# Two banded layers: the band in four 64x64 tiles with crossed channels, part of the inner norm on VectorE, and another order within a step

## The chip, the core and the metric

The kernel runs on one core of a Trainium2 chip. The metric is the device time of one execution in microseconds (us). It is given as the median of several runs of the same program. A profile is taken of one execution apart from these.

The core has five engines that run side by side, each with its own queue of instructions worked off in order: TensorE (PE in the profile; its weight loads are a row of their own, PEld), VectorE (DVE), ScalarE (ACT), GpSimd (POOL) and SyncE (SP), which here issues nearly all transfers. TensorE writes to PSUM, a memory of eight banks; a tile called "banks" takes two of them, a tile called "bank" takes one.

## The reference

The input is x of shape 1x512x512x64 in float32. Two identical layers with weights of their own act on it one after the other, each preceded by a group norm over pairs of channels. One layer, with WIN = 4, 64 channels in and 128 inside:

```
xn    = layernorm(x) * norm_scale + norm_bias
left  = (xn @ Wl + bl) * mask * sigmoid(xn @ Wlg + blg)
right = (xn @ Wr + br) * mask * sigmoid(xn @ Wrg + brg)
gate  = sigmoid(xn @ Wog + bog)
out[i, j, c] = sum over k = i-4 .. i+4 of  left[k, i, c] * right[k, j, c]
y     = (layernorm(out) * out_norm_scale + out_norm_bias) * gate @ Wo + bo
```

The sum over k is a banded matrix product for each of the 128 channels c: rows i of the result need rows i-4 to i+4 of `right`. The result of a layer is added to its input.

## The kernel before

**Rows and columns.** The 512 rows are cut into nine blocks of S = 64 rows that overlap by eight (`row_blocks`). A block's 512 columns come as two halves of 256, which stand on partitions 0 to 63 and 64 to 127 at the same time. A *chunk* is 128 columns of each half, so there are 18 chunks in a layer. A chunk is worked in 16 *units* of JU = 8 columns. The loop in `layer` (lines 765 to 847) makes one *step* t per unit. In one step, different units are in different stages.

**Stages.** A unit is loaded (`load`), gets the group norm (`affine`, two GpSimd operations over 128x512 elements), its statistics (`inner_stats`, VectorE) and the inner layer norm (`inner_norm`, lines 435 to 439, two GpSimd operations over 128x512). TensorE transposes it (`transposed`) and ScalarE copies the result from PSUM to the tile zT (`kept`, line 460), which is also stored to DRAM (`later`). `right` (line 487) projects a unit in two calls of four columns: TensorE, a sigmoid on ScalarE into `sg`, a product on VectorE into RO. `left` (line 497) does so for the nine diagonals that the band needs, once in each layer in its first steps, and writes them to DRAM (`left_of`).

**Band.** When a chunk's 16 units are in RO, `mix` (line 539) multiplies: one call takes HB = 8 channels, that is 16 calls in a chunk. A stationary operand is a 64x64 matrix of `left` for a channel, taken from a slab A of HA = 16 channels that `take_left` (line 527) has fetched; the moving operand is RO, 64 rows of 128 columns. Each call uses two 64x64 tiles of the array: rows 0 to 63 with output partitions 0 to 63, and rows 64 to 127 with output partitions 64 to 127. Half of a call's result goes back to RO by ScalarE, half by VectorE. The 16 calls fall on ten of a chunk's 16 steps: 2, 1, 2, 2, 1, 2, 1, 2, 2, 1 (line 729).

**Output.** Some 14 steps after a chunk is complete each unit goes out: `out_stats` (VectorE), `norm` (line 610, eight ScalarE operations), `gates` (line 622, TensorE and two sigmoids), `turned` (line 641: transposes, then the product with the gate on VectorE into ZH), `end` (line 673: output projection, VectorE's sum with the input XR, two stores). `biased` adds a constant to XR on GpSimd. In layer one `sums` collects channel sums on TensorE for the group norm of the next layer. `solve` (line 577), every fourth step, turns the variances of several units into reciprocal roots: a few small VectorE operations and some dozen small ones on GpSimd; `norm` and `inner_norm` of the next steps use its results (`nm`, `rs`).

**Order.** Everything issued through `en` keeps the order of the program text on its engine, so the lines of the loop are the queue order of each engine. Two tiles of two banks (`two_banks`) are shared, in turn, by the two calls of `right`, by `transposed` and by each `mix`; whoever takes one waits until the one before has been read out. Single banks (`one_bank`) go round among three in layer one and four in layer two. In the profile nearly every line of the loop is recorded as L373, the wrapper that keeps the order, so groups are told apart by their tiles.

Of the kernel before, what the change touches and what calls it, by code (L numbers as in the profile page):

```python
# [8 lines left out]
F32 = mybir.dt.float32  # L9
I32 = mybir.dt.int32  # L10
AF = mybir.ActivationFunctionType
# [5 lines left out]
P = 128  # L17
WIN = 4
# [7 lines left out]
HB = 8  # L26
HA = 16
# [52 lines left out]
def tile_two_banded_layers(  # L80
# [27 lines left out]

    slab = S * (S + 2 * WIN) * HA
    size = H // HA * slab  # L110
# [271 lines left out]
    class Unit:  # L382
# [4 lines left out]
        def __init__(self, at: int, blk: Block = None, j: int = 0, near: int = None):  # L387
            self.at, self.blk, self.j, self.near = at, blk, j, near

# [45 lines left out]
    def inner_norm(u: Unit):  # L435
        z = u.z.rearrange("p (k t) c -> p k t c", t=2)
        m = u.mean.unsqueeze(3).broadcast_to([P, JU // 2, 2, D])
        en.gpsimd.tensor_tensor(z, z, m, ALU.subtract)
        en.gpsimd.tensor_tensor(u.z, u.z, last(u.rs, D), ALU.mult)
# [20 lines left out]
    def kept(u: Unit):  # L460
        u.t = ztp.tile([P, JU // 2, P], F32, tag="zT", name="zT")
        to = u.t.rearrange("c k (n p) -> c n k p", n=2)
        for n, pt in enumerate(u.pt):
            en.scalar.activation(
                to[:, n : n + pt.shape[1]], pt.rearrange("c n (k p) -> c n k p", p=S),
                AF.Identity, bias=1.0,
            )
        if u.near is None:
            en.sync.dma_start(later[u.at], u.t)
# [5 lines left out]
    def projected(u: Unit, q: int, w: bass.AP):  # L475

        pr = two_banks().rearrange("p (e k h) -> p e k h", e=2, k=JQ // 2)
        for k in range(JQ // 2):
            for e in range(2):
                part = slice(e * D, (e + 1) * D)  # L480
                en.tensor.matmul(
                    pr[:, e, k, :], lhsT=u.t[part, q // 2 + k, :], rhs=w[part],
                    start=True, stop=True,
                )
        return pr

    def right(u: Unit, q: int, w: dict):
        pr = projected(u, q, w["right"]).rearrange("p e k h -> p (e k) h")
        sg = wk.tile([P, JQ, H], F32, tag="sg", name="sg", bufs=2)
        en.scalar.activation(sg, pr[:, :, H:], AF.Sigmoid)  # L490
        en.vector.tensor_tensor(
            RO[:, :, u.c + q : u.c + q + JQ, :],
            pr[:, :, :H].rearrange("p j (h t) -> p h j t", t=2),
            sg.rearrange("p j (h t) -> p h j t", t=2), ALU.mult,
        )

    def left(u: Unit, q: int, w: dict):

        n0 = u.near + q
        pr = projected(u, q, w["left"])  # L500
        sg = wk.tile([P, JQ, H], F32, tag="sg", name="sg", bufs=2)
        sl = sg.rearrange("p j h -> p (j h)").rearrange("p (s j x) -> p s j x", j=JQ, x=HA)
        sv = sl.rearrange("p s (k e) x -> p e k s x", e=2)
        for e in range(2):
            en.scalar.activation(
                sv[:, e], pr[:, e, :, H:].rearrange("p k (s x) -> p k s x", x=HA), AF.Sigmoid
            )
        near = w["near"][:, n0 : n0 + JQ].unsqueeze(1).unsqueeze(3)
        en.gpsimd.tensor_tensor(sl, sl, near.broadcast_to([P, H // HA, JQ, HA]), ALU.mult)
        for e in range(2):  # L510
            en.vector.tensor_tensor(
                sv[:, e], pr[:, e, :, :H].rearrange("p k (s x) -> p k s x", x=HA), sv[:, e],
                ALU.mult,
            )
        for o, r, k, m in runs(n0, n0 + JQ):
            for n, b in enumerate(blocks):
                q0 = b.s // JQ
                at = n * size + (r * (S + 2 * WIN + 1) + k) * HA
                en.sync.dma_start(
                    strided(  # L520
                        left_of, at, (JQ * (S + 2 * WIN + 1) * HA, S // JQ), (slab, H // HA),
                        (1, m * HA),
                    ),
                    sl[q0 : q0 + S // JQ, :, o : o + m, :].rearrange("q s j x -> q s (j x)"),
                )

    def take_left(n: int, h: int) -> bass.AP:


        A = lp.tile([P, S, HA], F32, tag="A", name="A")  # L530
        at = n * size + h * slab + WIN * HA
        for e in range(2):
            en.sync.dma_start(
                A[e * S : (e + 1) * S].rearrange("p i h -> p (i h)"),
                strided(left_of, at, ((S + 2 * WIN) * HA, S), (1, S * HA)),
            )
        return A

    def mix(c: int, A: bass.AP, h0: int):


        j0 = c % 2 * (JC - JW)
        R = RO[:, :, j0 : j0 + JC, :]
        pb = two_banks()
        ph = pb.rearrange("i (h j) -> i h j", j=JC)
        for turn in range(2):
            for h in range(HB // 2):
                for e in range(2):
                    part = slice(e * S, (e + 1) * S)
                    hh = (turn ^ e) * (HB // 2) + h  # L550
                    en.tensor.matmul(
                        ph[part, hh, :], lhsT=A[part, :, h0 % HA + hh],
                        rhs=R[part, (h0 + hh) // 2, :, hh % 2],
                        start=True, stop=True,
                    )
        q = HB // 4
        for n in range(2):
            o = R[:, h0 // 2 + n * q : h0 // 2 + (n + 1) * q]
            v = pb.rearrange("i (h t j) -> i h j t", t=2, j=JC)[:, n * q : (n + 1) * q]
            if n == 0:  # L560
                en.scalar.copy(o, v)
            else:
                en.vector.tensor_copy(o, v)
# [46 lines left out]
    def norm(o: Out):  # L610
        o.on = onp.tile([P, JU, H], F32, tag="on", name="on")
        for j in range(JU):
            en.scalar.activation(
                o.on[:, j, :].rearrange("p (h t) -> p h t", t=2), RO[:, :, o.c + j, :],
                AF.Identity, bias=o.nm[:, j : j + 1], scale=o.rs[:, j : j + 1],
            )
# [5 lines left out]
    def gates(o: Out, w: dict):  # L622
# [3 lines left out]
        for e, pg in enumerate(pgs):  # L626
            part = slice(e * D, (e + 1) * D)
            en.tensor.matmul(
                pg, lhsT=w["gate"][part],
                rhs=o.t[part].rearrange("c k (e p) -> c (k e) p", e=2)[:, :, b.lo : b.hi],  # L630
                start=True, stop=True,
            )
        g = gp.tile([H, 4 * JQ * (S - WIN)], F32, tag="gate", name="gate")
        for e, pg in enumerate(pgs):
# [6 lines left out]
    def turned(o: Out, w: dict):  # L641
# [10 lines left out]
        for n, pt in enumerate(pts):  # L652
# [20 lines left out]
    def end(dst: bass.AP, o: Out, w: dict):  # L673
        m = o.blk.m
        po = one_bank().rearrange("i (j c) -> i j c", c=D)
        for k in range(JQ):
            for e in range(2):
                for n in range(2):
# [5 lines left out]
                    )  # L684
        f = o.xr[: S + m, :, 1 : 1 + 2 * D]
# [18 lines left out]
    def layer(src: bass.AP, dst: bass.AP, w: dict, stats: bool, then=None):  # L704
# [60 lines left out]
        for t in range(min(loads), last_t + 3):  # L765
# [22 lines left out]
            for v in looking[:3]:  # L788
                out_stats(*v)

            for u in affines.pop(t, []):
                affine(u, en.vector if u.at < NU + 4 else en.gpsimd)
            if t % 4 == 0 and t > NU:
                then_affine = affines.pop(t + 1, [])

# [11 lines left out]
            if t in units:  # L807
                right(units[t], 0, w)
            for v in looking[3:5]:
                out_stats(*v)  # L810
            if t in outs:
                gates(outs[t], w)
            if t in units:
                right(units[t], JQ, w)
            if t in lefts:
                for q in range(0, min(JU, NEAR * JQ - lefts[t].near), JQ):
                    left(lefts[t], q, w)
            for u in inputs(t + 2):
                inner_norm(u)
            if t in outs:  # L820
                turned(outs[t], w)
            for u in inputs(t + 1):
                transposed(u)
                kept(u)
            if t in outs:
                biased(outs[t], w, stats)
            for v in looking[5:]:
                out_stats(*v)
            for v in todo:
                inner_stats(*v)  # L830
            if t - 1 in outs:
                end(dst, outs[t - 1], w)
            if stats and t - 2 in outs:
                sums(outs[t - 2], t - 2 == first_t, t - 2 == last_t)
            if t % 4 == 0:
# [3 lines left out]
                for u in then_affine:  # L839
                    affine(u, en.gpsimd)  # L840
                then_affine = []
                if us or os:
                    solve(w, us, os, st, so)
            if t + 1 in outs:
                norm(outs[t + 1])
            for n, (c, h0) in enumerate(mixes.get(t, [])):
                mix(c, A[c, h0 // HA], h0)
# [76 lines left out]

    XR = [keep.tile([P, JU // 2, 2 * D + 2], F32, name=f"XR{i}") for i in range(4)]
# [56 lines left out]
```

## Time and profile before

Three runs took 4958.12, 4958.66 and 4960.42 us. The profiled execution has a span of 4957.7 us.

| stretch | us | PE | DVE | ACT | POOL | PE clock |
|---|---|---|---|---|---|---|
| layer one, up to its first norm | 300 to 526 | 145.56 | 132.36 | 72.48 | 165.25 | 0.80 |
| layer one, first to last norm | 526 to 2621 | 1975.11 | 1657.60 | 1747.31 | 1743.03 | 0.99 |
| between | 2621 to 2884 | 150.43 | 158.61 | 75.12 | 167.42 | 0.79 |
| layer two, first to last norm | 2884 to 4947 | 1888.43 | 1671.47 | 1745.09 | 1743.69 | 0.98 |

The columns of engines are busy times in us. The stretch ahead of 300 us is the group norm's statistics of the input. [...] The costliest groups of the page, with the number of instructions, busy time and the mean of one:

| engine, work | number | busy us | mean ns |
|---|---|---|---|
| ACT norm (on<-RO) | 4608 | 1872.5 | 496 |
| PE projections (banks<-pack,zT) | 9360 | 1325.0 | 405 |
| PE band (banks<-RO,A) | 18432 | 1154.3 | 277 |
| DVE output statistics (sto<-RO) | 2304 | 842.8 | 413 |
| DVE right product (RO<-banks,sg) | 1152 | 789.9 | 686 |
| POOL affine, two operations | 2x536 | 687.8 and 687.1 | 1283 and 1282 |
| POOL inner norm, two operations | 2x586 | 627.2 and 618.0 | 1070 and 1055 |

The mean times the number is more than the busy time where instructions overlap in their engine's pipeline.

### The profile page before, as it was taken

What the parts mean: (1) busy time and instruction counts of PE and PEld (TensorE: products, weight loads), DVE (VectorE), ACT (ScalarE), POOL (GpSimd) and SP (SyncE); (2) the same over time, 40 slices, a digit from 0 to 9 for tenths busy, and PEclk for the clock granted to TensorE, in tenths of its full rate; (3) what the DMA queues carried; (4) which work ended last, traced back from release to release, by engine and by line L of the source; (5) the groups of instructions that cost most, each with busy time, mean ns of one, the idle gap of its engine ahead of it and who ended that gap; (6) DMA issues with size and microseconds to landing.
All of it is one profiled execution on the core that took longest, in us unless ns stands there. A gap on an engine that the chain in (4) does not pass through costs nothing. (4 is left out here: it accounts for less than half of the span.)

```text
span 4957.7 us, 173298 instructions
## 1 busy us (share of the span) xinstructions
PE 4186.4 (84%) x67090; PEld 3543.6 (71%) x67090; DVE 3836.3 (77%) x9635; ACT 3645.2 (74%) x8156; POOL 3826.5 (77%) x4739
## 2 busy tenths in 40 slices
PE   1036899999999999999974689999999999999998
PEld 0025788888888888888763577777777777777775
DVE  6855788888888888888766578888888888888876
ACT  0013788888888888888872378888888888888888
POOL 0037888888888888888534788888888998889853
PEclk6558999999999999999996899999999999999999
DMA  7844677777777777777653467777777777777765
GB/s 305 338 156 130 182 203 207 204 207 204 204 203 204 205 206 206 202 207 210 187 143 88 129 181 205 202 207 205 203 206 202 205 206 205 208 207 209 209 184 152
DMA packets 905343, 982.32 MB, mean 198 GB/s; under 512 B 114210, under 2 KB 641608, under 8 KB 900168
## 3 DMA queue, kind: packets, MB, share of 16 engines
q1 hardware_dynamic: 899840, 969.73, 66.9%
q8 instruction: 531, 8.70, 0.8%
q14 instruction: 292, 2.39, 0.2%
q10 hardware_dynamic: 4680, 1.50, 0.1%
HBM read 658.42 MB, written 312.46 MB: 196 GB/s over the span
## 5 line engine op out<-in xcount | busy, mean ns | idle before, releaser
L373 ACT ACTIVATE on<-RO,nm,rs 128x128 f32<-128x128 f32 x4608 | 1872.5, 496 | 130.1 <-POOL nm L373 110.3
L373 PE MATMUL banks<-pack,zT 64*128 64x256 f32 x9360 | 1325.0, 405 | 148.6 <-DVE RO L373 67.8
L373 PEld LDWEIGHTS banks<-pack,zT 64*128 64x128 f32 x9360 | 886.7, 194 | 517.6 <-DVE RO L373 220.1
L373 PE MATMUL banks<-RO,A 64*64 64x128 f32 x18432 | 1154.3, 277 | 12.7 <-ACT zT L373 12.7
L373 DVE TENSOR_TENSOR RO<-banks,sg 128x512 f32<-128x512 f32 x1152 | 789.9, 686 | 421.1 <-ACT sg L373 402.9
L373 PEld LDWEIGHTS banks<-RO,A 64*64 64x64 f32 x18432 | 1082.3, 183 | 38.6 <-ACT zT L373 15.2
L373 ACT ACTIVATE sg<-banks 128x512 f32<-128x512 f32 (+1 forms) x1188 | 695.0, 587 | 372.5 <-PE banks L373 288.6
L373 DVE BATCH_NORM_STATS2 sto<-RO 128x6 f32<-128x256 f32 x2304 | 842.8, 413 | 1.2
L373 DVE SCALAR_TENSOR_TENSOR ZH<-bank,pack,gate 128x448 f32<-128x448 f32 (+1 forms) x1152 | 738.4, 683 | 71.5 <-ACT gate L373 46.9
L373 DVE COPY RO<-banks 128x512 f32<-128x512 f32 x576 | 396.3, 691 | 487.6 <-ACT RO L373 487.0
L373 POOL TENSOR_TENSOR z<-z,gb 128x512 f32<-128x512 f32 x536 | 687.1, 1282 | 42.0
L373 PE MATMUL bank<-pack,ZH 128*64 128x64 f32 x18432 | 682.8, 229 | 6.1 <-ACT gate L373 5.6
L373 POOL TENSOR_TENSOR z<-z,ga 128x512 f32<-128x512 f32 x536 | 687.8, 1283 | 0.1
L373 POOL TENSOR_TENSOR z<-z,rs 128x512 f32<-128x512 f32 x586 | 618.0, 1055 | 46.0
L373 PEld LDWEIGHTS bank<-pack,ZH 128*64 128x64 f32 x18432 | 602.1, 141 | 48.2 <-ACT gate L373 9.6
L373 POOL TENSOR_TENSOR z<-z,sti 128x512 f32<-128x512 f32 x586 | 627.2, 1070 | 0.0
L373 ACT ACTIVATE gate<-bank 128x448 f32<-128x448 f32 (+1 forms) x1152 | 565.9, 543 | 81.1 <-PE bank L373 66.9
L373 PEld LDWEIGHTS bank<-ident,on 64*128 64x128 f32 x9216 | 409.7, 140 | 260.5 <-ACT gate L373 145.3
L373 PE MATMUL bank<-ident,on 64*128 64x64 f32 x9216 | 450.2, 227 | 137.9 <-ACT gate L373 107.3
L373 PE MATMUL bank<-zg,pack 64*128 64x448 f32 (+1 forms) x2304 | 559.5, 558 | 2.2 <-DMA zg<-later 1.5
L373 POOL TENSOR_TENSOR XR<-XR,pack 120x512 f32<-120x512 f32 (+1 forms) x352 | 418.4, 1190 | 160.6 <-DMA XR<-in_x_dram 58.9
L373 ACT COPY RO<-banks 128x512 f32<-128x512 f32 x576 | 333.5, 583 | 234.1 <-PE banks L373 234.0
(145 smaller groups left out, 3683.3 us busy)
## 6 DMA issues: line engine op xcount, KB each, us to landing
later<-zT SPq DMA_DIRECT2D x576, 256.0 KB
A<-left_of SPq DMA_DIRECT2D x576, 256.0 KB
zg<-later SPq DMA_DIRECT2D x576, 256.0 KB
z<-in_x_dram SPq DMA_DIRECT2D x576, 128.0 KB
z<-mid_x SPq DMA_DIRECT2D x576, 128.0 KB
gn_x<-in_x_dram SPq DMA_DIRECT2D x16, 4096.0 KB
XR<-in_x_dram SPq DMA_DIRECT2D x448, 112.0 KB
mid_x<-XR SPq DMA_DIRECT2D x448, 112.0 KB
```

Source lines behind the costliest of these rows:

```text
L373: return lambda *a, **k: tc.keep_in_program_order(f(*a, **k))
```

## The change

It has four parts.

1. **Band.** `mix` uses all four 64x64 tiles. The channels are taken in two halves s (0 to 63 and 64 to 127). For s = 0 the tiles are those of before; for s = 1 rows 0 to 63 give output partitions 64 to 127 and the other way round. So that the second half's result stands right, its right-hand side is put into RO crossed: `crossed` replaces `projected` in `right` and issues each projection as two matmuls of 128 columns, with the stationary operand shifted by 64 for s = 1. zT is 192 columns wide for this, the third 64 a second copy of the first 64, which `kept` makes with one more ScalarE operation per unit.
2. **Left.** The products of `left` go to L9, a part of RO not yet in use, and from there to DRAM in rows of 72 bytes (36 transfers in a layer). A slab A is laid out by channel pair and comes in pieces of 512 bytes, by four transfers in place of two.
3. **Inner norm.** GpSimd's two operations cover six of a unit's eight columns (from the second chunk on); two VectorE operations, one for each of the first ZV = 2 columns, subtract and multiply in one.
4. **Order.** `right`, `gates`, `turned` and `end` are split into their TensorE, ScalarE and VectorE parts, `norm` into two halves, and the loop issues these in another order.

```diff
+ZV = 2
...
     def inner_norm(u: Unit):
-        z = u.z.rearrange("p (k t) c -> p k t c", t=2)
-        m = u.mean.unsqueeze(3).broadcast_to([P, JU // 2, 2, D])
-        en.gpsimd.tensor_tensor(z, z, m, ALU.subtract)
-        en.gpsimd.tensor_tensor(u.z, u.z, last(u.rs, D), ALU.mult)
+        n = ZV if u.at > NU else 0
+        m = last(u.mean.rearrange("p k t -> p (k t)")[:, n:], D)
+        en.gpsimd.tensor_tensor(u.z[:, n:], u.z[:, n:], m, ALU.subtract)
+        en.gpsimd.tensor_tensor(u.z[:, n:], u.z[:, n:], last(u.rs[:, n:], D), ALU.mult)
+
+    def inner_norm_v(u: Unit):
+        for j in range(ZV if u.at > NU else 0):
+            en.vector.tensor_scalar(
+                u.z[:, j], u.z[:, j], u.mean[:, j // 2, j % 2 : j % 2 + 1], u.rs[:, j : j + 1],
+                ALU.subtract, ALU.mult,
+            )
...
         if u.near is None:
-            en.sync.dma_start(later[u.at], u.t)
+            en.scalar.activation(
+                to[:, 2], u.pt[0][:, 0].rearrange("c (k p) -> c k p", p=S), AF.Identity, bias=1.0
+            )
+            en.sync.dma_start(later[u.at], u.t[:, :, :P])
...
+    def crossed(u: Unit, q: int, w: bass.AP):
+
+        pr = two_banks().rearrange("p (e k h) -> p e k h", e=2, k=JQ // 2)
+        for k in range(JQ // 2):
+            for s in range(2):
+                for e in range(2):
+                    part = slice(e * D, (e + 1) * D)
+                    en.tensor.matmul(
+                        pr[:, e, k, :].rearrange("p (g s x) -> p g s x", g=2, s=2)[:, :, s],
+                        lhsT=u.t[part, q // 2 + k, s * S : s * S + P],
+                        rhs=w[part].rearrange("c (g s x) -> c g s x", g=2, s=2)[:, :, s],
+                        start=True, stop=True,
+                    )
+        return pr
...
-        A = lp.tile([P, S, HA], F32, tag="A", name="A")
-        at = n * size + h * slab + WIN * HA
-        for e in range(2):
-            en.sync.dma_start(
-                A[e * S : (e + 1) * S].rearrange("p i h -> p (i h)"),
-                strided(left_of, at, ((S + 2 * WIN) * HA, S), (1, S * HA)),
-            )
+        A = lp.tile([P, HA // 2, S, 2], F32, tag="A", name="A")
+        q = HA // 4
+        for e in range(2):
+            for s in range(2):
+                en.sync.dma_start(
+                    A[e * S : (e + 1) * S, s * q : (s + 1) * q].rearrange("p h i t -> p h (i t)"),
+                    strided(
+                        left_of, n * size + (s * H // 4 + h * q) * span + 2 * WIN,
+                        (H // 2 * span, S), (span, q), (1, 2 * S),
+                    ),
+                )
...
-        for turn in range(2):
-            for h in range(HB // 2):
-                for e in range(2):
-                    part = slice(e * S, (e + 1) * S)
-                    hh = (turn ^ e) * (HB // 2) + h
-                    en.tensor.matmul(
-                        ph[part, hh, :], lhsT=A[part, :, h0 % HA + hh],
-                        rhs=R[part, (h0 + hh) // 2, :, hh % 2],
-                        start=True, stop=True,
-                    )
+        ph = pb.rearrange("i (s h t j) -> i s h t j", s=2, h=q, t=2)
+        for h in range(q):
+            for t in range(2):
+                for s in range(2):
+                    for e in range(2):
+                        part, to = (slice(n * S, (n + 1) * S) for n in (e, e ^ s))
+                        en.tensor.matmul(
+                            ph[to, s, h, t, :], lhsT=L[part, s, h, :, t], rhs=R[part, s, h, :, t],
+                            start=True, stop=True,
+                        )
+        return [(R[:, s], ph[:, s].rearrange("i h t j -> i h j t")) for s in range(2)]
```

The order of a step, each line with the engines that it issues to (`looking` is the list of output statistics due in the step, `todo` that of the inner ones):

```
before                                        after
out_stats looking[:3]          DVE            left (first steps only)
affine                         POOL           gates               PE
right 0                        PE ACT DVE     right 0             PE
out_stats looking[3:5]         DVE            affine              POOL
gates                          PE ACT         right JQ            PE
right JQ                       PE ACT DVE     gated               ACT
left (first steps only)                       right_gate 0        ACT
inner_norm                     POOL           out_stats [0:2]     DVE
turned                         PE DVE         inner_norm          POOL
transposed, kept               PE ACT SP      out_stats [2:5]     DVE
biased                         POOL           inner_stats todo    DVE
out_stats looking[5:]          DVE            turned              PE
inner_stats todo               DVE            out_stats [5:]      DVE
end                            PE DVE SP      solve (every 4th)   DVE POOL
sums                           PE             right_gate JQ       ACT
affine of the next (every 4th) POOL           biased              POOL
solve (every 4th)              DVE POOL       right_end 0, JQ     DVE
norm 0 to 8                    ACT            times_gate          DVE
mix, its two copies            PE ACT DVE     norm 0 to 4         ACT
mix, its two copies            PE ACT DVE     end                 PE
                                              inner_norm_v        DVE
                                              affine of the next  POOL
                                              sums                PE
                                              transposed          PE
                                              mix                 PE
                                              kept                ACT SP
                                              its ScalarE copy    ACT
                                              mix                 PE
                                              its ScalarE copy    ACT
                                              ended               DVE SP
                                              VectorE copy, first DVE
                                              norm 4 to 8         ACT
                                              VectorE copy, 2nd   DVE
```

## The prediction

> **What bounds the kernel now.** I read the page's busy times first, then busy time stretch by stretch over one chunk of layer one (16 steps, cut where ScalarE starts the norm of a step), then the timeline of one such step, then the groups kept apart by shape.
>
> ```profile
> PE 4186.4 (84%) x67090; PEld 3543.6 (71%) x67090; DVE 3836.3 (77%) x9635; ACT 3645.2 (74%) x8156; POOL 3826.5 (77%) x4739
> ```
>
> Four engines between 74% and 84%: the average names no bound. The stretches do (columns: stretch, its length, then busy time of PE, PEld, DVE, ACT, POOL, the granted clock, DMA share and GB/s):
>
> ```profile
> 1253.14:1258.84 5.70, 5.24 (x100) 4.29 (x97) 4.79 (x11) 5.55 (x14) 5.24 (x5) 1.00 0.73 216
> 1267.80:1274.97 7.17, 7.17 (x132) 6.30 (x129) 5.92 (x16) 6.31 (x15) 7.01 (x6) 1.00 0.73 213
> 1274.97:1283.94 8.97, 8.97 (x164) 8.12 (x161) 6.53 (x16) 6.89 (x17) 8.73 (x9) 1.00 0.71 204
> 1283.94:1292.90 8.96, 8.96 (x164) 8.12 (x160) 7.35 (x21) 6.88 (x16) 8.72 (x9) 1.00 0.76 211
> 1353.17:1360.70 7.53, 7.09 (x136) 6.01 (x133) 6.85 (x21) 5.65 (x15) 5.73 (x15) 1.00 0.81 239
> sum 118.92, PE 113.79 PEld 99.47 DVE 96.75 ACT 100.15 POOL 106.33; mean PE 7.11 PEld 6.22 DVE 6.05 ACT 6.26 POOL 6.65
> ```
>
> A step without a band call takes 5.7 us and ScalarE fills 5.55 of it; with one call 7.17, with two 8.97, and there TensorE is busy all the time. A chunk has six steps with two calls, four with one, six with none. The last stretch has no call and takes 7.53: it follows a solve, and the waits put 110.3 us in all down to ScalarE's norm waiting for GpSimd's `nm`. Layer two is alike (118.17 us a chunk) with TensorE at 107.94, having no channel sums.
>
> ```profile
> 1275.92 3.94 PE L373 MATMUL banks<-RO,A 64*64 64x128 f32 x64
> 1278.12 0.57 ACT L373 COPY RO<-banks 128x512 f32<-128x512 f32 x1
> 1278.72 0.69 DVE L373 COPY RO<-banks 128x512 f32<-128x512 f32 x1 [1.18 <-ACT RO L373]
> 1279.79 1.13 PE L373 MATMUL banks<-pack,zT 64*128 64x256 f32 x8
> 1281.51 1.03 PE L373 MATMUL banks<-pack,zT 64*128 64x256 f32 x8
> 1282.37 0.69 PE L373 MATMUL bank<-ident,on 64*128 64x64 f32 x16
> 1283.34 1.15 PE L373 MATMUL bank<-pack,ZH 128*64 128x64 f32 x32
> ```
>
> Two band calls are 64 matmul instructions in 3.94 us, 1.97 each, and each VectorE copy of a band half follows its ScalarE copy.
>
> **The band.** Both diagonal tiles run at once: single records start in pairs every 113.5 ns, 16 pairs a call. The change issues the same 32 instructions in fours. Lower end: 8 x 113.5 ns plus the 0.17 that a last matmul trails, 1.08 alone, 0.95 in a run. Next row: the output projection, also 32 instructions, two column tiles over the same rows, took 1.15 with 64 columns each, so instructions can be fed that fast and two column halves do stream at once. Upper end: no gain, 1.97. I take 1.05: **0.92 off TensorE per call**, 14.7 a chunk.
>
> [...] In the new loop the two row halves of one `s` write one bank, in different partitions. [...]
>
> **The right projection** becomes 16 instructions of 128 columns for 8 of 256 per call: equal columns. Pairs now start 216 ns apart under weight-load records of 187. Lower end 0; upper end, if a load of 187 bounds each of the 8 pairs: 1.50 for 0.86, so +0.64 a call. The transposes (16 in 0.69, loads of 138 ns, 86 ns a pair) show that such a record is mostly latency. I take +0.05 a call, +0.1 a step.
>
> **The third copy of zT on ScalarE**, per unit:
>
> ```profile
> L373 ACT ACTIVATE zT<-banks 128x512 f32<-128x512 f32 x542 | 324.1, 598 | 95.8 <-PE banks L373 67.9 <-DMA XR<-in_x_dram 2.6
> L373 ACT ACTIVATE zT<-bank 128x256 f32<-128x256 f32 x88 | 29.0, 385 | 160.9 <-PE bank L373 123.0 <-DMA later<-zT 35.3 <-issue 2.5
> L373 DVE TENSOR_SCALAR nm<-sto 128x32 f32<-128x32 f32 x144 | 25.2, 175 | 0.0
> L373 DVE TENSOR_SCALAR rs<-var 128x64 int32<-128x64 int32 x128 | 25.0, 195 | 0.0
> ```
>
> 128x256 costs 385 ns by itself; by the difference of the two shapes 213 is the part that queued work can't hide. I take 0.30. Nothing hides it in steps without a band call, where ScalarE was the bound.
>
> **Inner norm.** GpSimd's two operations (1070 and 1055 ns) go over six of eight columns: -0.53 a step, 106.3 to 97.9 a chunk. VectorE gains two 128x64 operations: 175 (128x32) to 282 (the slowest row of this kind); I take 195, nearest in shape: **+0.39 a step**. They stand between the gate product and the output sum; behind them queue that sum and the band copies, which TensorE's next projections await. [...]
>
> **Transfers.** A slab comes in 512-byte pieces, four issues for two, zT is stored likewise. Packets of 512 B took 28.8 ns on average, those of 4096 B 253.7: eight cost 230, nothing more. SP's issues of 512-byte rows (XR) took 0.5 each: 16 more a chunk, 8 us of a queue that uses some 60. SP's order stays: loads, slab, recall, zT store, result. Slabs are called two band calls or more ahead, which hides them; late, the band would wait. The left band's writes lose the hold on `sg`: ScalarE waited for them 33.9 and 33.4 us in the two fills.
>
> **The order.** The solve moves ahead of the right products on VectorE and ahead of `biased` on GpSimd, its user `norm` one step on, so the solve stall (about 1.9 us in the 7.53 step, 0.8 in another) goes. New waits: VectorE's right products stand behind 2.8 us of statistics, and both two-bank buffers stay taken until then; TensorE covers with gates, both projections, turning, output projection and sums (0.75+0.92+0.92+0.5+0.94+0.46 = 4.5 us). The second band call waits for `kept`, whose buffer it takes, and ScalarE's second copy waits for it.
>
> **The sum**, per step, by the engine that then binds:
> - no call: ScalarE 5.55+0.30 = 5.85, VectorE up to 5.58+0.39 (its longest such stretch): **6.0** (before 5.7).
> - one call: ScalarE 6.31+0.30 = 6.6, VectorE up to 6.20+0.39: **6.7** (before 7.2).
> - two calls: TensorE 8.97-1.84+0.1 = 7.2; ScalarE 6.89+0.30 = 7.2, plus about 0.4 left of the wait between `kept` and the second copy (1.05 less the first copy's 0.57): **7.6** (before 8.9).
>
> 6x7.6 + 4x6.7 + 6x6.0 = 108.4. The four solves put 0.65 us more in VectorE's queue ahead of the right products: 111.0. Against (118.9+118.2)/2 = 118.5 that is -7.5 a chunk. From the first to the last norm of each layer are 2095 and 2063 us, 35 chunks: **-263**. The fills: -20 of the 67 that waited for `sg`. 4957.7 - 283 = **4675** for the profiled execution, whose span lies 1 us under the median 4958.66: I leave it.
>
> **Rivals.**
> 1. *Half the gain.* The records of ScalarE laid end to end instead of overlapped: norms 3.25, gates 0.98, two sigmoids 1.20, `kept` 0.96, second band call 1.13, copy 0.57: 8.1 with two calls, 7.0 with one, 6.35 with none. 48.6+28+38.1 = 114.7, -3.8 x 35 = -133: **4825**. For: ScalarE and VectorE hand to each other four times a step. Against: in 5.7 us steps ScalarE was 97% busy with as many hands. The right projection's upper end gives as much: TensorE at 8.3 in two-call steps.
> 2. *Slower: the right products behind the statistics.* Steps that carry eight inner statistics have 3.9 to 4.3 us on VectorE ahead of them. Once statistics plus one product (0.69) exceed the 4.5 us cover, TensorE idles holding both buffers, and the loop last copy, statistics, product, transposes (0.45), `kept` (0.8), second call (1.13), copies (0.57+0.69) closes at 8.6 us. If VectorE enters a step late by 0.4 each time, steps are 9.0, 7.5, 6.6: 54+30+39.6 = 123.6, +5.1 x 35 = +179: **5135**. Against: VectorE idled 487.0 us for ScalarE's copies, time it can start early with.
> 3. *The four tiles don't run together.* At the old pace the chunk is 6x9.1+4x7.3+36 = 119.8 in layer one and 116.9 in layer two: **4955**. At 2.05 us a call it turns to a loss; waiting out each 272 ns matmul record would make 4.35 a call, and some 6300.
> 4. *Better.* ScalarE alone sets the pace at 100.2+16x0.30 = 105 a chunk: **4470**.
>
> **Chances.** Forecast 0.55, its own range 4580 to 4750; half the gain 0.25; better 0.04; no change 0.03; slower 0.13, of it the statistics 0.09 and the tiles 0.04. So faster by over 0.2% 0.84, within 0.2% (10 us, what can't be told from no change) 0.03, slower 0.13. The range 4540 to 4860 leaves the slow side and the best out; its ends come from the band call at 0.95 with VectorE's pieces at 0.175, and from rival 1 with the small operations at 0.28.
>
> **What would show it.** Band calls of about 1.0 us in quads; right projections at 1.1; two-call steps near 7.6 and empty steps near 6.0, ScalarE over 90% busy; no norm waiting for `nm`; GpSimd near 3520 busy, VectorE near 4060, TensorE near 3720. Wrong if a band call stays near 2, if a right projection exceeds 1.4, or if TensorE's waits for VectorE's RO grow well over the 220 us they are now.

## The result, and the profile after

The changed kernel takes 4837.32 us (median, 4828.45 to 4842.72) beside 4959.54 of the kernel before in the same job: a ratio of 0.9751, interval [0.9737, 0.9765], 122 us faster. The forecast was 4675, 283 faster, with a range of 4540 to 4860. So the sign is right and the time lies in the range, but 162 us of the gain are missing. The profiled execution spans 4835.3 us.

The page's busy times, as shown of before (there VectorE had 77%):

```profile
PE 3858.8 (80%) x76306; PEld 3246.6 (67%) x76306; DVE 4360.2 (90%) x10719; ACT 3745.5 (77%) x8732; POOL 3599.2 (74%) x4739
```

VectorE's busy time has grown by 524 us; 225 were forecast. Stretches of a chunk of layer one (stretch, length, busy time of PE, PEld, DVE, ACT, POOL, granted clock, DMA share, GB/s): no band call, one call, two calls, one with two calls and a solve, and the sum over all 16 steps.

```profile
1347.73:1353.41 5.68, 5.50 (x103) 4.75 (x100) 5.68 (x11) 5.68 (x15) 5.52 (x7) 1.00 0.45 133
1374.05:1381.12 7.07, 6.12 (x134) 5.18 (x132) 7.07 (x16) 6.47 (x17) 6.91 (x7) 1.00 0.77 210
1405.10:1413.98 8.88, 7.21 (x166) 5.96 (x164) 8.88 (x22) 7.24 (x17) 8.57 (x9) 1.00 0.73 199
1428.77:1437.42 8.65, 7.90 (x192) 6.76 (x190) 7.19 (x23) 6.99 (x18) 6.20 (x15) 1.00 0.79 217
sum 116.04, PE 105.75 PEld 90.83 DVE 113.10 ACT 103.59 POOL 97.42; mean PE 6.61 PEld 5.68 DVE 7.07 ACT 6.47 POOL 6.09
```

TensorE's 113.8 us of 118.9 have fallen to 105.75; in the second and third lines VectorE is busy from end to end where TensorE was before. The bound has changed engines. Over one step with two band calls, the timeline (start, length, engine, operation, count, idle before and what ended it):

```profile
1263.50 2.18 PE L374 MATMUL banks<-RO,A 64*64 64x128 f32 x64
1263.61 0.87 ACT L374 ACTIVATE zT<-banks 128x512 f32<-128x512 f32 x2 [0.17 <-PE banks L374]
...
1266.46 1.95 PE L374 MATMUL banks<-pack,zT 64*128 64x128 f32 x32
```

Two band calls are 64 matmuls in 2.18 us, 1.09 each (1.97 before); the single records start in fours, one four every 113 ns or so; before they started in pairs, as far apart. Two right projections are 32 matmuls in 1.95, 0.98 each (1.03 to 1.13 before); both zT copies take 0.87, 0.27 more than one. And the groups of the inner norm, kept apart by shape (busy us, mean ns of one | idle before):

```profile
L374 DVE TENSOR_SCALAR z<-z,sti,rs 128x64 f32<-128x64 f32 x1084 | 657.1, 647 | 0.0
...
L374 POOL TENSOR_TENSOR z<-z,sti 128x384 f32<-128x384 f32 x542 | 456.6, 842 | 0.0
L374 POOL TENSOR_TENSOR z<-z,rs 128x384 f32<-128x384 f32 x542 | 454.1, 838 | 42.5
```

GpSimd's pieces shrank to 842 and 838 ns (1070 and 1055 before). VectorE's operations of one column take 647 ns each, not 195. The timeline shows why:

```profile
1217.45 1.26 POOL L374 TENSOR_TENSOR z<-z,gb 128x512 f32<-128x512 f32 x1
1218.23 1.34 DVE L374 TENSOR_SCALAR z<-z,sti,rs 128x64 f32<-128x64 f32 x2
1218.68 0.84 POOL L374 TENSOR_TENSOR z<-z,sti 128x384 f32<-128x384 f32 x1
1219.59 0.83 POOL L374 TENSOR_TENSOR z<-z,rs 128x384 f32<-128x384 f32 x1
1222.40 0.18 DVE L374 TENSOR_SCALAR var<-var 128x32 f32<-128x32 f32 x1
```

The pair starts at 1218.23 under a GpSimd instruction and ends at 1219.57; the next GpSimd instruction ended at 1219.52. At 1222, with GpSimd idle, short operations of the solve take 0.16 to 0.18. Taken over the whole trace by whether a GpSimd instruction overlaps, 29 of the 1084 operations have none beside them and take 305 ns (median); the other 1055 take 657 on average, 95% of them up to 1305, and 798 end within 120 ns after a GpSimd instruction does. VectorE's statistics of z (276 ns alone, 278 beside) and its output sum, which reads PSUM (681 and 679), show no such thing.

The warning was in the trace of before, in two rows of short operations:

```profile
L373 DVE TENSOR_SCALAR var<-sti 128x32 f32<-128x32 f32 x136 | 38.4, 282 | 0.1
L373 DVE TENSOR_SCALAR var<-var 128x32 f32<-128x32 f32 x144 | 34.8, 241 | 4.9
```

The second, with a mean of 241 ns, is 135 records of 181 ns and 9 beside a GpSimd instruction of 1143.

### The profile page after: what moved, and what is told of

Same layout as the page of the kernel before. It is cut to its first block, busy times and chain, and to the rows that moved or that the text cites. A ratio compares the mean times of both kernels' runs of the same rounds, so it can differ in the third digit from the quotient of the medians.

```text
span 4835.3 us, 193356 instructions
## 1 busy us (share of the span) xinstructions
PE 3858.8 (80%) x76306; PEld 3246.6 (67%) x76306; DVE 4360.2 (90%) x10719; ACT 3745.5 (77%) x8732; POOL 3599.2 (74%) x4739
## 4 chain that ended last, share of the span: by engine, by line
PE 39%; DVE 30%; DMA 11%; POOL 6%; issue 5%; ACT 5%; SPq 3%; ACTq 0%; DVEq 0%; POOLq 0%
PE banks L374 20%; PE bank L374 19%; DVE RO L374 8%; DVE z L374 6%; DVE ZH L374 5%; ACT on L374 3%; POOL z L374 3%; SPq L374 3%; DVE gn_st L374 3%; DVE sto L374 3%; DMA zg<-later 2%; DVE XR L374 2%; DVE sti L374 2%; DMA mid_x<-XR 1%; POOL rsqrt L374 1%
## 5 line engine op out<-in xcount | busy, mean ns | idle before, releaser
L374 PEld LDWEIGHTS banks<-pack,zT 64*128 64x128 f32 x18576 | 1251.7, 195 | 562.5 <-DVE RO L374 304.7
L374 PE MATMUL banks<-pack,zT 64*128 64x128 f32 x18576 | 1359.7, 287 | 318.9 <-DVE RO L374 205.3
L374 DVE TENSOR_TENSOR RO<-banks,sg 128x512 f32<-128x512 f32 (+1 forms) x1188 | 753.1, 672 | 242.6 <-ACT sg L374 119.5
L374 PE MATMUL banks<-RO,A 64*64 64x128 f32 x18432 | 632.2, 281 | 37.8 <-DVE RO L374 6.5
L374 DVE TENSOR_SCALAR z<-z,sti,rs 128x64 f32<-128x64 f32 x1084 | 657.1, 647 | 0.0
L374 PEld LDWEIGHTS banks<-RO,A 64*64 64x64 f32 x18432 | 531.4, 136 | 89.4 <-DVE RO L374 68.7
L374 ACT ACTIVATE zT<-banks 128x512 f32<-128x512 f32 (+1 forms) x1084 | 470.6, 488 | 134.4 <-PE banks L374 120.2
L374 POOL TENSOR_TENSOR z<-z,rs 128x384 f32<-128x384 f32 (+1 forms) x586 | 508.1, 867 | 45.9
L374 POOL TENSOR_TENSOR z<-z,sti 128x384 f32<-128x384 f32 (+1 forms) x586 | 512.8, 875 | 0.0
L374 DVE BATCH_NORM_STATS2 sti<-z 128x6 f32<-128x128 f32 x2344 | 500.0, 278 | 0.7 <-DMA left_of<-RO 0.5
```

The lines of the kernel that those rows point to most:

```text
L374: return lambda *a, **k: tc.keep_in_program_order(f(*a, **k))
```

## The experiments

Each theory's numbers were written before its run. Ratios are to the kernel before in the same job (4953 to 4958 us).

**1. The inner norm back on GpSimd.**

```diff
-ZV = 2
+ZV = 0
```

> The changed kernel with ZV = 0: all eight columns of the inner norm on GpSimd again. Theory W (each small VectorE operation stands until GpSimd's instruction is through, 647 ns each, and so VectorE bounds the step): VectorE busy falls by the 657 us of these operations to about 3700, GpSimd rises to about 3825, TensorE's waits for VectorE's RO fall below 400 us from 575, and the time falls by 120 to 200 us, to 4640 to 4720, GpSimd then being the fullest engine. Theory O (the hand-overs of the new order set the pace and the small operations only fill idle VectorE time): within 20 us of the changed kernel, 4820 to 4860, with VectorE idle more.

Measured 4779.71 us, 0.9643 [0.9628, 0.9659]: 58 faster than with two columns, so the edit that was to help costs time. That is more than theory O allows and less than half of what theory W gave: VectorE's busy time fell to 3947 us, not to 3700. Most steps without a solve take what was forecast (7.57 with two calls, 6.43 with one in layer one). But steps that hold a solve take up to 10.2 us. The solve's short operations on VectorE now stand beside a GpSimd that is busy 107.3 of 115 us (1200 to 1315): in the chunk from 1235 us `var<-var` takes 0.9 to 1.2 us in three steps of 8.5 to 10.2, and 0.18 in one of 5.7. Over the run (groups by shape):

```profile
L374 DVE TENSOR_SCALAR var<-var 128x32 f32<-128x32 f32 x144 | 104.4, 725 | 5.0
```

**2. The same two columns in the two-source form.**

```diff
-            en.vector.tensor_scalar(
+            en.vector.scalar_tensor_tensor(
...
+                u.rs[:, j : j + 1].broadcast_to([P, D]), ALU.subtract, ALU.mult,
```

> The changed kernel with the two small operations as scalar_tensor_tensor (subtract the mean, multiply by the reciprocal root read as a broadcast tensor) in place of tensor_scalar; same columns, same place. Theory W, if the wait belongs to the one-source form: records of about 250 to 300 ns in place of 647, VectorE busy about 4000, time 4640 to 4720. If any VectorE operation with all operands in SBUF waits so, or theory O holds: records above 500 ns or an unchanged time near 4835.

Measured 4826.15, 0.9738 [0.9723, 0.9752], with 637 ns each, above the 500 of the second case:

```profile
L374 DVE SCALAR_TENSOR_TENSOR z<-z,sti,rs 128x64 f32<-128x64 f32 x1084 | 648.4, 637 | 0.0
```

The delay doesn't belong to the one-source form.

**3. One column** (`ZV = 1`).

> The changed kernel with ZV = 1: one column by VectorE, seven by GpSimd. Theory W: one record of about 600 ns a step, half of the loss back, 4730 to 4780. Theory O: 4820 to 4860.

Measured 4781.03, 0.9652 [0.9633, 0.9671]. This is 1 us above theory W's range: half the operations at 585 ns each, and VectorE falls to 4137.0 us busy. Taking both columns away gains no more than taking one: something else holds these two.

**4. The four tiles without the new order** (band, crossed projection, third copy and transfers as changed; the sequence of a step as before; no column on VectorE). Its core:

```diff
             if t in units:
+                right(units[t], 0, w)
+                right_gate(units[t], 0)
+                right_end(units[t], 0)
...
+            for c, h0 in mixing:
+                two = mix(c, A[c, h0 // HA], h0)
+                en.scalar.copy(*two[0])
+                en.vector.tensor_copy(*two[1])
```

> The band in four tiles with crossed channels, the third copy and the new left transfers, but the order of the kernel before and no norm work on VectorE (ZV = 0). If the band alone frees TensorE as its records say (1.10 us a call for 1.97): steps with two calls fall from 8.9 to about 7.7, steps without one rise by 0.3, the solve stalls stay: 4730 to 4800. If the four tiles need the new order to be of use: 4900 or more.

Measured 5155.1, 1.0402 [1.0386, 1.0417]: the second of the two cases, and slower even than before. Two steps with two calls, and the largest waits:

```profile
1311.42:1320.27 8.85, 7.10 (x179) 6.35 (x176) 6.34 (x16) 7.08 (x18) 8.62 (x8) 1.00 0.74 200
1363.59:1372.48 8.89, 7.10 (x179) 6.35 (x176) 6.55 (x21) 7.06 (x17) 4.02 (x13) 1.00 0.75 204
```

```profile
DVE RO L374 <- ACT sg L374: 724.7, 734, 16.2
PE banks L374 <- DVE RO L374: 716.2, 455, 16.6
```

No engine sets this length: GpSimd is nearly full in the first of the two and half idle in the second, the others are at 6.3 to 7.1 in both. TensorE, ScalarE and VectorE wait for each other in turn. At the same columns on VectorE (none), the order is worth 5155 - 4780 = 375 us. In the old order the four tiles, with their copy and transfers, cost 197 us; they only pay when the hand-overs are moved apart. The new order without the four tiles was not run, so what it is worth by itself stays open.

**5. The solve's short operations to GpSimd** (on top of run 1).

```diff
-            en.vector.tensor_scalar(vo, vo, LN_EPS, None, ALU.add)
+            en.gpsimd.tensor_scalar(vo, vo, LN_EPS, None, ALU.add)
...
-        rsqrt(r, v, en.vector, en.gpsimd)
+        rsqrt(r, v, en.gpsimd, en.gpsimd)
```

> All of the inner norm back on GpSimd, as in the run with no column on VectorE (4779.71 us), and besides the solve's short operations that were VectorE's (the first on the variance, the added epsilon, the first integer operation of the root, together 1.9 to 2.7 us in a solve there, 725, 522 and 401 ns each) moved to GpSimd. Theory W (a short VectorE operation stands until the GpSimd instruction under way ends, and the delay passes to the right products): the long steps of 9 to 10.8 us that hold a solve fall to about 8, two of four in a chunk by 1 to 2 us, 35 chunks: 4640 to 4720; GpSimd about 110 us a chunk. Rival (these operations are simply that long, or GpSimd's own queue sets the solve steps): 4780 or more, since GpSimd was already at 106.3 us a chunk.

Measured 4888.54, 0.9862 [0.9849, 0.9875]: the rival, and 109 slower than run 1. Nearly every chunk of layer one takes 116.8 us, and ScalarE's norm waits 223.9 us for GpSimd's `nm`. The solve merely left one queue for a fuller one.

**6. A quieter GpSimd** (two columns on VectorE). The kernel leaves out the group norm's `affine` on GpSimd, a part of the computation.

```diff
-                affine(u, en.vector if u.at < NU + 4 else en.gpsimd)
+                if u.at < NU + 4:
+                    affine(u, en.vector)
...
-                affine(u, en.gpsimd)
+                pass
```

> The changed kernel with the affine step of the group norm left out on GpSimd (its two operations per unit, a part of the computation that is left out, kept only in the first units where VectorE does it), so that GpSimd has its inner-norm pieces and little else. Theory W: the 128x64 norm operations of VectorE, 647 ns each now, start less often beside a running GpSimd instruction and fall to 300 to 480; VectorE's busy time falls by 150 to 350 us, and the kernel to 4650 to 4780. Rival (the operation is that long by its own shape or its per-channel scalars): still over 600 ns each and 4800 to 4840.

Measured 4804.75, 0.9696 [0.9683, 0.971], a time in the rival's range, but with the one-column operations where theory W put them:

```profile
L374 DVE TENSOR_SCALAR z<-z,sti,rs 128x64 f32<-128x64 f32 x1084 | 391.5, 402 | 0.0
```

The same instruction falls from 647 to 402 ns when only GpSimd's work changes: this settles that it is GpSimd's work that holds it. Those still beside a GpSimd instruction take 452 on average, the rest 305. The solve's operations are back at 0.16 to 0.20 us, and the solve step that took 10.2 in run 1 takes 6.5. But the time fell by 33 us only. TensorE now waits 207.7 us for `zg`, in the longest steps above all (11.1 us at 1304), and the fills grew, as in all four kernels of this job (see run 8).

**7. The left band's call later**, where it stood before.

```diff
-            if t in lefts:
-                for q in range(0, min(JU, NEAR * JQ - lefts[t].near), JQ):
-                    left(lefts[t], q, w)
...
                 right_end(units[t], JQ)
+            if t in lefts:
+                for q in range(0, min(JU, NEAR * JQ - lefts[t].near), JQ):
+                    left(lefts[t], q, w)
```

> The changed kernel with the call that writes the left band placed behind the end of the right products again, where it stood before; it acts only in the first 11 steps of a layer. Theory F (the fills gained nothing because the left band's GpSimd copies now stand ahead of what VectorE waits for: VectorE's RO copies wait 117.9 us for GpSimd's sg): that wait falls to 60 to 90 and the time by 15 to 35 us. Rival (the fill waits for the transfers of zT and of the slabs, or for the same copies wherever they stand): within 8 us of the changed kernel's 4837.

Measured 4890.76, 0.9866 [0.9852, 0.9879]: 53 slower than the changed kernel, a miss of both theories. Its two fills (up to the first norm of each layer) are 23 and 22 us longer. Part of that belongs to the job (see run 8): beside runs 5, 6 and 8 they are 11 to 15 and 7 to 14 longer. So the place that I suspected is worth some 20 to 30 us as it is.

**8. Two transfers to a slab instead of four** (two columns on VectorE).

```diff
-            for s in range(2):
-                en.sync.dma_start(
-                    A[e * S : (e + 1) * S, s * q : (s + 1) * q].rearrange("p h i t -> p h (i t)"),
+            en.sync.dma_start(
+                A[e * S : (e + 1) * S].rearrange("p (s h) i t -> p s h (i t)", s=2),
...
-                        (H // 2 * span, S), (span, q), (1, 2 * S),
+                    (H // 2 * span, S), (H // 4 * span, 2), (span, q), (1, 2 * S),
```

> The changed kernel with each slab of A fetched in two transfers of 256 KB as before the change, in the same 512-byte pieces, instead of four: 576 issues for 1152. Theory Q (SP's queue of 691 ns an issue, 796 us in all against 316 before, delays the loads behind it): TensorE's waits for zg fall from 43 to under 20 us and the time by 10 to 40 us. Rival (the queue has slack, the wait for zg comes of the transfers themselves): within 8 us of 4837.

Measured 4851.71, 0.9795 [0.9782, 0.9809], 14 slower than the changed kernel, which neither theory gave. The wait did what theory Q said, from the first line to the second (waits of TensorE, after and this run):

```profile
PE bank L374 <- DMA zg<-later: 43.4, 39, 5.1
```

```profile
PE bank L374 <- DMA zg<-later: 4.0, 2, 3.8
```

and the time didn't. From the first to the last norm the layers take 2023.8 and 1989.0 us, 2031.5 and 1993.6 without this edit: 12 us in all, so with VectorE full little of TensorE's wait counts. What was lost lies in the fills, 12 and 11 us longer, and need not come of the edit: runs 5, 6 and 7, of the same job, leave the slabs alone and their first norm is late as well (544.4 to 559.2 us; 548.3 here, 535.9 in the changed kernel). In these four an issue of the left band's writes takes 1.52 to 1.57 us, in all other runs with these writes 1.28 to 1.35. Why, the traces don't show.

**9 to 12. Both limits lifted.** One column on VectorE, together with the slab in two transfers (9), or the load of `zg` called ahead of the slab's (10), or both (12); and both with no column (11).

```diff
-            for c, h in slabs.get(t, []):
-                A[c, h] = take_left(c // per, h)
             if t + 2 in outs:
                 recall(outs[t + 2])
+            for c, h in slabs.get(t, []):
+                A[c, h] = take_left(c // per, h)
```

What they take away is seen in run 3 (timeline, SPq is the queue of SP):

```profile
1318.45 2.59 SPq L374 DMA_DIRECT2D A<-left_of  x4
1321.13 0.55 SPq L374 DMA_DIRECT2D zg<-later  x1
...
1325.08 1.35 PE L374 MATMUL bank<-zg,pack 64*128 64x448 f32 x4 [2.96 <-DMA zg<-later]
```

> One column of the inner norm on VectorE (4781.03 us alone) and each slab in two transfers. Theory Q2 (two limits stand one behind the other: with two columns VectorE's 113 us of 116 a chunk hide that the loads of zg come late; with one column TensorE's wait for zg, 80.0 us, is part of the time, and half the slab issues take it away as they did at two columns, 43.4 to 4.0): wait for zg under 15 us, long steps shorter, 4690 to 4745. Rival (the wait only moves to another engine, or the fills grow): 4765 or more.

> One column on VectorE, four transfers to a slab, but the load of zg issued ahead of the slab's transfers in a step instead of behind them. Theory Q2: what makes zg late is the 2.6 us of slab issues ahead of it, so the wait for zg falls from 80.0 to under 25 us and the time to 4710 to 4760. Rival (SP's queue as a whole runs late, 96 us of issues in a chunk of 114, whatever the order): wait over 50 us and 4765 or more.

> No column on VectorE (4779.71 us alone), a slab in two transfers, and the load of zg ahead of the slab's. Theory Q2: wait for zg from 72.8 to under 10 us, 4690 to 4740; the solve steps, 9 to 10 us by VectorE's short operations beside a full GpSimd, stay. Rival: 4765 or more.

> One column on VectorE, a slab in two transfers, and the load of zg ahead of the slab's. Theory Q2: wait for zg under 10 us, 4680 to 4735, the best of the four or equal to the run with two transfers alone within 10 us. Rival: 4765 or more.

Measured 4729.53 (0.955 [0.9537, 0.9563]), 4730.3 (0.9549 [0.9536, 0.9562]), 4745.75 (0.9578 [0.9565, 0.9591]) and 4723.23 (0.9535 [0.9522, 0.9548]): three within what theory Q2 gave, run 11 six above its end, none at the rival's 4765 or more. TensorE's wait for `zg` is 8.8 us in run 9 and 6.1 in run 10, of 80.0 in run 3. The two edits replace each other; either is worth 51, both 58.

**13. The first stores of zT on a queue of their own** (on top of 12). In the changed kernel's fill, ScalarE stands 15 us for a store that is issued behind the left band's writes:

```profile
373.29 7.97 SPq L374 DMA_DIRECT2D left_of<-RO  x3
381.36 1.70 SPq L374 DMA_DIRECT2D later<-zT  x1
...
391.57 0.66 ACT L374 ACTIVATE zT<-bank 128x256 f32<-128x256 f32 x2 [15.36 <-DMA later<-zT]
```

```diff
-            en.sync.dma_start(later[u.at], u.t[:, :, :P])
+            (en.scalar if u.at < 12 else en.sync).dma_start(later[u.at], u.t[:, :, :P])
```

> The best kernel so far (one column on VectorE, a slab in two transfers, zg ahead of the slab: 4723.23 us) with the stores of zT of the first twelve units of a layer issued from ScalarE's queue, not behind the left band's writes in SP's. Theory F2 (in the fills ScalarE waits up to 15 us a time for a store of zT that stands behind the left band's writes in one queue, 79.5 us in all): that wait falls under 25 and the time by 15 to 45 us, 4680 to 4708. Rival (the left band's small pieces keep the transfer engines themselves busy, so that the store is as late from any queue, or the wait moves back to sg): within 8 us of 4723.

Measured 4704.2, 0.9493 [0.948, 0.9506]: the best run, 133 us under the changed kernel. ScalarE's wait, in run 12 and here:

```profile
ACT zT L374 <- DMA later<-zT: 79.5, 8, 15.4
```

```profile
ACT zT L374 <- DMA later<-zT: 30.9, 8, 7.8
```

The time is in the range, and all of the gain lies in the fills. The wait stayed above 25; what holds the rest of it was not separated. A chunk of this run: no call, one call, two calls, a solve step with one call, one with two, and the sum. In the first of the solve steps TensorE's granted clock is 0.83, but TensorE is busy 7.57 of 10.00 us only.

```profile
1203.11:1208.81 5.70, 5.52 (x104) 4.76 (x102) 4.63 (x10) 5.70 (x16) 5.54 (x7) 1.00 0.72 214
1222.30:1228.72 6.42, 6.39 (x143) 5.45 (x141) 6.42 (x16) 6.32 (x17) 6.26 (x6) 1.00 0.94 248
1236.30:1243.87 7.57, 7.48 (x178) 6.44 (x176) 7.48 (x19) 6.89 (x17) 7.41 (x7) 1.00 0.86 222
1243.87:1253.87 10.00, 7.57 (x141) 6.43 (x138) 9.13 (x23) 6.40 (x16) 8.94 (x18) 0.83 0.76 187
1275.50:1284.82 9.32, 7.50 (x179) 6.52 (x177) 7.65 (x20) 7.00 (x18) 7.91 (x17) 1.00 0.88 226
...
sum 112.43, PE 106.85 PEld 92.80 DVE 106.15 ACT 101.81 POOL 102.71; mean PE 6.68 PEld 5.80 DVE 6.63 ACT 6.36 POOL 6.42
```

**14. The solve's short operations to GpSimd once more**, on top of 12, where GpSimd isn't full.

> The same kernel of 4723.23 us with the solve's short operations (on the variance, the added epsilon, the first integer operation of the root) moved from VectorE to GpSimd, as in the run of 4888.54, but with GpSimd at 103 us of 112 a chunk instead of full. Theory W: the solve steps, 10.0 and 9.0 us in layer one, lose the 1.5 us or so in which VectorE's operations stand for GpSimd and fall to 8 to 8.5; 4640 to 4700. Rival (the chain of the solve on GpSimd, some 0.3 us each and now longer, is what the steps wait for, through the inner norm and nm): 4725 to 4800.

Measured 4739.4, 0.9568 [0.9555, 0.9581]: the rival. The solve steps still take 10.2 and 9.4 us, and ScalarE waits 125.2 us for `nm`. That the operations stand for GpSimd was shown by run 6; that moving them helps is refuted. What holds these steps is open: in run 6 the step was short (6.5), but there GpSimd's own queue, in which the rest of the solve runs, was short too.

## Why the prediction had the sign right and the gain wrong

**Where the 162 us are.** From 4837.3: one column less gives 56 (run 3), `zg` on time 58 more (run 12), the stores of zT 19 (run 13), in this order, since the second is worth little before the first (run 8). 29 are left at 4704.2: 16 between the first and last norms of the layers (247 us shorter than before, 263 forecast), 13 in the fills.

**The step that failed first** is "VectorE gains two 128x64 operations: 175 to 282; I take 195, nearest in shape: +0.39 a step". They measured 647 each, 1.29 a step, 14.5 us more a chunk than forecast. The upper end was "the slowest row of this kind"; but a row is a mean, and 282 mixed records of 173 (median) with a top twentieth of 1223 to 1259. So it bounded nothing: the operation mostly lasted until the GpSimd instruction it met had ended (798 of the 1055 that met one). VectorE became the bound (113.10 of 116.04), and not by the statistics of rival 2. The place of the pair, between gate product and output sum, passed the delay on: TensorE's waits for VectorE's RO grew from 132.9 to 378.3 us and those of its weight loads from 220.1 to 574.6, the third of the signs of being wrong. That the time still lies in the range is luck: the upper end stood on rival 1 and on small operations of 0.28 us, and neither came.

Runs 1, 2 and 6 show the waiting: 725 ns (`var<-var`), 637 and 402 (`z`). The statistics show none, 278 beside GpSimd and 276 alone. What in the hardware makes the operation wait, no run shows. Even alone it takes 305, more than the 282 of the upper end.

**The second** is the transfers: "eight cost 230, nothing more" and "16 more a chunk, 8 us of a queue that uses some 60". Summed over the issue records, SP's queue held 72 us a chunk before and 96 after: a slab's issue grew from 549 ns to 691 although it carries half the bytes, with twice as many. The load of `zg` ended its issue 11.0 us ahead of its first matmul on average before, and 6.0 after. I asked whether the slab would come late ("the band would wait") and not who is queued behind it: SP's order, which I had listed, has the recall right there. Hidden behind VectorE, this costs some 12 us in the changed kernel (run 8), and 50 as soon as VectorE is relieved.

**The third** is "the fills: -20". They grew by 10 and 6. The hold on `sg` did go; in its place ScalarE waits 90.6 us for the store of zT, behind the left band's writes of 1.33 us each. Run 13 shows this for 19 us of it. Run 7 shows that the earlier call saves some 20 to 30; what else in the fills takes time stays open.

**The solve**: its stall went (ScalarE's waits for `nm`: 110.3 to 1.5 us), but "0.65 us more in VectorE's queue" for each of four solves is, in the best run, some 3.6 and 1.8 for two of them, in steps of 10.00 and 9.32 beside 6.42 and 7.57. What holds them is open (run 14).

**What held**: the band call (1.05 forecast, 1.09), the right projection (no slower: 0.98), the third copy (0.30; 0.27), GpSimd's pieces, and, once VectorE and SP are out of the way, the steps themselves: 7.57, 6.42 and 5.7 to 6.0 for 7.6, 6.7 and 6.0, and a chunk of 112.4 for 111.0. Rival 1 named the time well (4825) by a mechanism that is not the one found, a coincidence: it lays ScalarE's records end to end, 8.1 us with two calls, and run 13 has 7.57. Rival 2 fell: run 13 has the same statistics ahead of the right products, and its steps take 7.57, 6.42 and 5.7 to 6.0, not 9.0, 7.5 and 6.6. Rival 3 fell (1.09 a call); its sum gives 4951, not 4955.

## What to carry to other kernels

Before work moves to an engine, split the rows that price it by what the neighbouring engine does at that moment: a mean of 241 ns that is made of 181 and 1143 is a warning, not an upper bound. When a step's transfers are split, list what stands behind them in the same queue, and how long before its use it is now issued. Test a suspected second limit with the first one lifted; with VectorE full, run 8 alone would have cleared the queue wrongly. And compare stage by stage with runs of the same job: the total of run 8 hid a gain between the norms behind fills that were long in all four kernels of its job.

## What the runs showed of the hardware

- The short VectorE operation from SBUF to SBUF on z, 128x64, mostly ended with the GpSimd instruction beside it (798 of 1055 within 120 ns after one): it took 305 ns alone and 657 on average beside, up to 1372; the two-source form 271 and 645 (run 2). Statistics (276 and 278) and the sum that reads PSUM (681 and 679) took the same alone and beside. `nm<-sto`, which follows right behind such an operation, was no longer beside (176 and 169 in the changed kernel).
- Two row halves wrote different partitions of one PSUM bank at once, where in the kernel before each had a bank of its own: the band's matmuls started in fours, 32 of them in 1.09 us where pairs took 1.97.
- What an issue of a slab by SP takes went with the layout and hardly with the amount: 549 ns for 256 KB in pieces of 4096 bytes, 691 for 128 KB in 512-byte pieces, and 715 for 256 KB in 512-byte pieces, twice as many (run 8; in run 13 two such issues took 1.29 us at 1244.44).
